# Where a two-layer graph-attention kernel asks whether its blocks hold all edges

## The chip, the cores and the metric

The kernel runs on one core of a Trainium2 chip. The metric is the device time of one execution in microseconds; the time before is the median of 3 runs. Beside it stands one execution taken by the hardware profiler, from which all durations are read.

## The reference

Two graph-attention layers over 3327 nodes with 1024 features, each with a residual and a layer norm. The adjacency matrix is sparse (a node has some 16 neighbours) and symmetric, with the diagonal set.

```python
h = x @ W                                    # layer 0: 8 heads of 128; layer 1: one head of 1024
e = leaky_relu(alpha_src[:, None] + alpha_dst[None, :], 0.2)
e = where(adj == 0, -inf, e)
out = softmax(e, axis=-1) @ h
x = layernorm(x + out)                       # layer 1: layernorm(x + relu(out))
```

## The kernel before, in words

The nodes are cut into 26 tiles of 128 rows (`NT = 26`, the last one partly filled). The program has three parts.

The first part is the stage "proj" (lines 453 to 699). For each tile, TensorE transposes x (`flip`, L176), multiplies it with the weights of layer 0 (`project`, L479), ScalarE copies the products out of PSUM (`keep`, L496), and SyncE writes them to the table `h0_d` in HBM (L499). Interleaved with this, the edges of each tile are turned into lists. The interleaving is written out by hand: `listing()` is a generator whose steps are called from `pace()` in the midst of the projections, so the order in each engine's queue is the order in which Python issues the instructions; nothing reorders them (`tc.manual_schedule()`). The steps that matter here:

- `words(t)` packs the adjacency rows and counts each node's edges (ScalarE L311, into `cnt[:, t, 0]`), four tiles ahead.
- `ends(t)` and `ends2(t)`, three tiles ahead of the lists, sum the counts over nodes: one small matmul each (L327, L346), a copy of it by ScalarE (L328, L347, into `cnt[:, t, 1]` and `cnt[:, t, 2]`) and a few small GpSimd operations.
- `keys` and `columns` find the column numbers of a tile's edges by repeated MAX8 and MATCH_REPLACE8 on VectorE (L274, L276).
- `places`, `give`, `take` and `sources` move these into blocks of edges: VectorE marks the places (L391, L392), TensorE permutes (L401, L411), ScalarE copies out (L423 to L428), and VectorE computes the index of each block's source rows (L436 to L450), into `idx`.

Behind the last list stands a question (L689 to L699): does every node have at most 32 edges, and does the spare block of each tile hold what is left over? VectorE scales the first count and copies the third into one tile `big`, reduces it to one number for each partition, TensorE transposes these 128 numbers (L695, into a PSUM bank of the tag "T", of which there are two, used in turn by `flip`, `ends`, `ends2` and this), VectorE reduces again and compares, and writes `flag`.

All five engines load the flag (L701) and branch on it (L1203). With the flag at 0, as with these inputs, the second part is `sparse`; the other arm, `by_pairs`, isn't run.

In `sparse`, layer 0 gathers the source rows of each tile's edges from `h0_d` with indirect DMAs from GpSimd (L803, four for each of four blocks and one for the spare block), VectorE makes the attention weights (L865 to L870), TensorE sums (L882 to L907), and the result is written to `y_d`. SyncE loads the lists' factors `re` (L812) and each tile's own rows (L838). Layer 1 does the same from `y_d` (L993), with its projection at the end (L1025).

The call that holds the order of the lists against the counts is in `listing`:

```python
                    if s == 3 and 2 < t + 3 < NT:
                        lists[t + 3].ends2(all_b)
                    yield
```

For t = 22 this is the last tile's second count; three lists (tiles 23, 24, 25) are then still to be finished.

Of the kernel before, what the change touches and what calls it, by code (L numbers as in the profile page):

```python
# [12 lines left out]
I32 = mybir.dt.int32  # L13
AF = mybir.ActivationFunctionType
OP = mybir.AluOpType
AX = mybir.AxisListType
# [3 lines left out]
P = 128  # L20
# [6 lines left out]
def kernel(  # L27
# [28 lines left out]
    nc = tc.nc  # L56
    N, D = x.shape
    H, DH = a0_src.shape
    NT = (N + P - 1) // P
# [8 lines left out]
    KMAX = 32  # L68
# [30 lines left out]
    const = ctx.enter_context(tc.tile_pool(name="const", bufs=1))  # L99
    scratch = ctx.enter_context(tc.tile_pool(name="scratch", bufs=1, space=DRAM))  # L100

    ident = const.tile([P, P], F32, name="ident")
# [10 lines left out]
    cnt = const.tile([P, NT, 3], F32, name="cnt")  # L113
# [43 lines left out]
    class Phase:  # L157
# [7 lines left out]
        def bank(self, tag, shape, name, dt=F32):  # L165
            return self.psum.tile(shape, dt, tag=tag, name=name, bufs=self.banks[tag])
# [286 lines left out]
    with ExitStack() as own, tc.manual_schedule():  # L453
        ph = Phase(own, "proj", {"A": 2, "S": 1, "T": 2})
        pool, bank = ph.pool, ph.bank
# [45 lines left out]
        def count(t):  # L501
            if t < NT:
                lists[t].words(ads.pop(t), junk)
                load_mask(t + 3)

        def listing():

            for t in range(-1, NT):
                old, new = lists[t] if t >= 0 else None, lists[t + 1] if t + 1 < NT else None
                for s in range(4):  # L510
                    if old:
                        old.give(s)
                    if new:
                        (new.keys, new.columns)[s // 2](s % 2)
                    if s == 1 and 2 < t + 3 < NT:
                        lists[t + 3].ends(tri_b)
                    if s == 3 and 2 < t + 3 < NT:
                        lists[t + 3].ends2(all_b)
                    yield
                if old:  # L520
                    old.give(EB)
                    old.take()
                count(t + 4)
                yield
                if old:
                    old.sources()
                    yield
                while new and t + 1 not in scored:
                    yield
                if new:  # L530
                    new.places()
                    yield

        scored, kept = set(), {}
        steps, slots, done = listing(), [0, 0], [0]

        def pace():
# [147 lines left out]
        for _ in steps:  # L685
            pass


        big = ph.sbuf("big", [P, NT, 2], 1)  # L689
        nc.vector.tensor_scalar(big[:, :, 0], cnt[:, :, 0], float(P) / KMAX, None, op0=OP.mult)  # L690
        nc.vector.tensor_copy(big[:, :, 1], cnt[:, :, 2])
        top = ph.sbuf("most", [P, 1], 1)
        nc.vector.tensor_reduce(top, big.rearrange("p a b -> p (a b)"), AX.X, OP.max)
        tr = bank("T", [1, P], "trc")
        nc.tensor.transpose(tr, top, ident)  # L695
        most = ph.sbuf("most1", [1, 1], 1)
        nc.vector.tensor_reduce(most, tr, AX.X, OP.max)
        flag = const.tile([1, 1], I32, name="flag")
        nc.vector.tensor_scalar(flag, most, float(P), None, op0=OP.is_gt)  # L699

    dense = nc.values_load(flag, min_val=0, max_val=1, skip_runtime_bounds_check_because="the result of a comparison")  # L701

# [529 lines left out]
```

## Time and profile before

| | us |
|---|---|
| median of 3 runs (1954.33 to 1958.33) | 1957.68 |
| the profiled execution | 1903.19 |
| its span, first to last instruction | 1901.5 |
| TensorE busy (share of the span) | 1518.5 (80%) |
| VectorE busy | 1146.6 (60%) |
| GpSimd busy | 1030.2 (54%) |
| ScalarE busy | 546.6 (29%) |

Times in the profile are in us from the first instruction. PE is TensorE's matmul queue, PEld its weight loads, DVE VectorE, ACT ScalarE, POOL GpSimd, SP SyncE, whose only work is to issue DMAs. A line such as L346 is a line of the kernel before. In the chain of waits each piece is work, or a wait for what released it; followed back from the last instruction, it tells what set the end. "issue" is time in which an engine waited for nothing that the profile shows. PEclk is the share of full clock that TensorE was granted. The ends of matmuls are modelled, so a gap of TensorE is known to some 0.1 us.

### The profile page before, as it was taken

What the parts mean: (1) busy time and instruction counts of PE and PEld (TensorE: products, weight loads), DVE (VectorE), ACT (ScalarE), POOL (GpSimd) and SP (SyncE); (2) the same over time, 40 slices, a digit from 0 to 9 for tenths busy, and PEclk for the clock granted to TensorE, in tenths of its full rate; (3) what the DMA queues carried; (4) which work ended last, traced back from release to release, by engine and by line L of the source; (5) the groups of instructions that cost most, each with busy time, mean ns of one, the idle gap of its engine ahead of it and who ended that gap; (6) DMA issues with size and microseconds to landing.
All of it is one profiled execution on the core that took longest, in us unless ns stands there. A gap on an engine that the chain in (4) does not pass through costs nothing.

```text
span 1901.5 us, 38079 instructions
## 1 busy us (share of the span) xinstructions
PE 1518.5 (80%) x14663; PEld 902.4 (47%) x14663; DVE 1146.6 (60%) x3058; ACT 546.6 (29%) x1422; POOL 1030.2 (54%) x1391
## 2 busy tenths in 40 slices
PE   8799999999266555656556565399999999999997
PEld 5465556666255554545545454144444444444443
DVE  6699999986386665666666666244444444444442
ACT  5544455542022222222222222012222212222220
POOL 4322222220576666676676764677766667666650
PEclk9899999999678777787788877699999999999999
DMA  7656455411899999999999997899999999999980
GB/s 184 101 133 131 100 99 99 88 62 39 325 373 404 396 392 394 366 405 392 386 392 389 394 376 273 332 398 410 400 372 382 380 378 369 359 371 373 366 326 33
DMA packets 171068, 567.76 MB, mean 299 GB/s; under 512 B 27690, under 2 KB 34346, under 8 KB 170878
## 3 DMA queue, kind: packets, MB, share of 16 engines
q0 software_dynamic: 131056, 455.68, 67.6%
q1 hardware_dynamic: 39822, 109.56, 15.4%
q8 instruction: 118, 1.93, 0.4%
q14 instruction: 72, 0.59, 0.1%
HBM read 578.85 MB, written 42.97 MB: 327 GB/s over the span
## 4 chain that ended last, share of the span: by engine, by line
PE 52%; DMA 24%; DVE 12%; ACT 6%; issue 4%; POOL 2%; SPq 0%; DVEq 0%; ACTq 0%; POOLq 0%
DMA src<-h_d,idx 20%; PE mm L1025 20%; PE acc L993 12%; PE mm L479 12%; DVE e L870 3%; PE acc L898 3%; ACT junk L311 3%; PE tr L176 2%; POOL src L803 2%; DMA src<-y_d,idx 2%; DVE pr L931 1%; PE acc L882 1%; DMA wt<-in_L_gnn_W_dram 1%; ACT xT L179 1%; PE xp L411 1%
## 5 line engine op out<-in xcount | busy, mean ns | idle before, releaser
L803 POOL DMA_INDIRECT src<-h_d,idx x416 | 441.1, 1060 | 209.1 <-PE acc L898 58.0
L803 POOL DMA_INDIRECT src<-y_d,idx x416 | 415.7, 999 | 221.6 <-PE acc L993 96.3
L898 PE MATMUL acc<-src,e 128*32 128x128 f32 x6656 | 278.5, 337 | 253.6 <-DVE e L870 253.5
L479 PE MATMUL mm<-wt,xT 128*128 128x347 f32 (+1 forms) x1248 | 402.3, 469 | 3.3 <-DMA wt<-in_L_gnn_W_dram 2.9
L1025 PE MATMUL mm<-wt,xT 128*128 128x512 f32 x832 | 383.3, 604 | 0.8 <-DVE o L1028 0.8
L898 PEld LDWEIGHTS acc<-src,e 128*32 128x32 f32 x6656 | 234.8, 137 | 311.3 <-DVE e L870 284.3
L479 PEld LDWEIGHTS mm<-wt,xT 128*128 128x128 f32 x1248 | 228.3, 192 | 106.0 <-issue 4.2
L1025 PEld LDWEIGHTS mm<-wt,xT 128*128 128x128 f32 x832 | 152.2, 190 | 199.5 <-issue 179.1
L993 PE MATMUL acc<-src,es 128*32 128x342 f32 (+1 forms) x2496 | 206.2, 464 | 33.8 <-DVE es L984 31.0
L870 DVE TENSOR_TENSOR e<-oh,way 128x1024 f32<-128x1024 f32 x130 | 158.7, 1221 | 63.2 <-ACT w L868 62.8
L993 PEld LDWEIGHTS acc<-src,es 128*32 128x32 f32 x2496 | 71.6, 111 | 158.6 <-issue 112.9
L868 ACT ACTIVATE w<-way 128x32 f32<-128x32 f32 (+1 forms) x130 | 24.6, 189 | 407.7 <-DVE way L866 395.6
L1028 DVE SCALAR_TENSOR_TENSOR o<-mm,y 128x512 f32<-128x512 f32 x52 | 35.9, 691 | 166.2 <-PE mm L1025 166.2
L1007 ACT ACTIVATE z<-y,ri 128x342 f32<-128x342 f32 (+1 forms) x78 | 39.5, 570 | 313.9 <-DVE ri L1003 313.9
L865 DVE TENSOR_TENSOR way<-src,re 128x32 f32<-128x32 f32 x104 | 20.8, 200 | 175.1 <-DMA src<-h_d,idx 157.6
L179 ACT ACTIVATE xT<-tr 128x512 f32<-128x512 f32 x104 | 59.4, 596 | 151.0 <-PE tr L176 150.9
L981 DVE TENSOR_TENSOR way<-way,src 128x128 f32<-128x128 f32 x104 | 31.1, 299 | 90.0 <-ACT way L951 44.2
L850 ACT ACTIVATE own<-own,es 128x128 f32<-128x128 f32 x208 | 63.6, 388 | 57.4 <-DVE es L847 57.4
L311 ACT ACTIVATE junk<-ad 128x3328 uint8<-128x3328 uint8 x26 | 78.4, 3014 | 2.5 <-POOL ad L308 2.5
L882 PE MATMUL acc<-end,e 128*128 128x128 f32 x416 | 67.7, 328 | 13.3 <-DVE e L870 13.3
L296 POOL CAST mvs<-r 128x8 bf16<-128x8 f32 x26 | 6.0, 232 | 122.8 <-ACT r L295 122.8
L335 POOL TENSOR_TENSOR place_of<-cnt 128x1 f32<-128x1 f32 x26 | 4.9, 190 | 121.0 <-ACT cnt L328 101.5
(188 smaller groups left out, 1959.7 us busy)
## 6 DMA issues: line engine op xcount, KB each, us to landing
h_d<-ht SPq DMA_DIRECT2D x26, 520.0 KB
own<-h_d SPq DMA_DIRECT2D x26, 520.0 KB
y_d<-y SPq DMA_DIRECT2D x26, 514.0 KB
y<-y_d SPq DMA_DIRECT2D x26, 514.0 KB
x<-in_x_dram SPq DMA_DIRECT2D x25, 512.0 KB
y<-in_x_dram SPq DMA_DIRECT2D x25, 512.0 KB
out_dram<-o SPq DMA_DIRECT2D x25, 512.0 KB
ad<-in_adj_dram POOLq DMA_DIRECT2D x25, 415.9 KB
```

Source lines behind the costliest of these rows:

```text
L176: nc.tensor.transpose(tr[:, k, :], src[:, (4 * g + k) * P : (4 * g + k + 1) * P], ident)
L179: nc.scalar.activation(part, tr, AF.Copy)
L311: nc.scalar.activation(junk, ad, AF.Copy, accum_out=self.deg)
L479: nc.tensor.matmul(acc, xT[t][:, k, :], wt[:, k, CUTS0[c] : CUTS0[c + 1]], start=k == 0, stop=k == KT - 1)
L803: nc.gpsimd.indirect_dma_start(out=s[:, g, :w], out_offset=None, in_=table[:, :], in_offset=bass.IndirectOffsetOnAxis(ap=idx[:, t, b * NG ...
L850: nc.scalar.activation(hn, hn, AF.Copy, scale=es[:, n : n + 1])
L870: nc.vector.tensor_tensor(e, oh.unsqueeze(2).to_broadcast([P, ng, H, wide]), wp.unsqueeze(3).to_broadcast([P, ng, H, wide]), OP.mult,)
L882: nc.tensor.matmul(self.acc[h // 4][:, h % 4, :], e[:, 0, h, :], rowsof[:, 0, h, :], start=False, stop=h % 4 == 3,)
L898: nc.tensor.matmul(self.acc[h // 4][g * GT : (g + 1) * GT, h % 4, :], e[:, g, h, :], rowsof[:, g, h, :], start=first and h % 4 == 0, stop= ...
L993: nc.tensor.matmul(self.acc[c][to, :m], es[:, g, :], s[:, g, CUTS[c] : CUTS[c + 1]], start=b == 0, stop=b == EB,)
L1007: nc.scalar.activation(z[:, cut], self.res[:, cut], AF.Copy, scale=ri[:, 1:2])
L1025: nc.tensor.matmul(acc, xT[:, k, :], wt1[:, k, half], start=k == 0, stop=k == KT - 1)
```

## The change

The operations of the question are put into a function `room()`, which is called in `listing` straight after `ends2` of the last tile. The block behind the last list is taken out. The load of the flag and the branch stay where they were, last in each engine's queue of the stage. Nothing else changes: on TensorE the transpose now stands between L346 and the eight transposes of the next `flip` (L176); on VectorE the five operations stand between the last MAX8 of tile 23's columns and L436 of tile 22; the queues of ScalarE, GpSimd and SyncE hold the same instructions in the same order.

```diff
                     if s == 3 and 2 < t + 3 < NT:
                         lists[t + 3].ends2(all_b)
+                        if t + 3 == NT - 1:
+                            room()
                     yield
...
+        flag = const.tile([1, 1], I32, name="flag")
+
+        def room():
+
+            big = ph.sbuf("big", [P, NT, 2], 1)
+            nc.vector.tensor_scalar(big[:, :, 0], cnt[:, :, 0], float(P) / KMAX, None, op0=OP.mult)
+            nc.vector.tensor_copy(big[:, :, 1], cnt[:, :, 2])
+            top = ph.sbuf("most", [P, 1], 1)
+            nc.vector.tensor_reduce(top, big.rearrange("p a b -> p (a b)"), AX.X, OP.max)
+            tr = bank("T", [1, P], "trc")
+            nc.tensor.transpose(tr, top, ident)
+            most = ph.sbuf("most1", [1, 1], 1)
+            nc.vector.tensor_reduce(most, tr, AX.X, OP.max)
+            nc.vector.tensor_scalar(flag, most, float(P), None, op0=OP.is_gt)
...
         for _ in steps:
             pass
 
-
-        big = ph.sbuf("big", [P, NT, 2], 1)
-        nc.vector.tensor_scalar(big[:, :, 0], cnt[:, :, 0], float(P) / KMAX, None, op0=OP.mult)
-        nc.vector.tensor_copy(big[:, :, 1], cnt[:, :, 2])
-        top = ph.sbuf("most", [P, 1], 1)
-        nc.vector.tensor_reduce(top, big.rearrange("p a b -> p (a b)"), AX.X, OP.max)
-        tr = bank("T", [1, P], "trc")
-        nc.tensor.transpose(tr, top, ident)
-        most = ph.sbuf("most1", [1, 1], 1)
-        nc.vector.tensor_reduce(most, tr, AX.X, OP.max)
-        flag = const.tile([1, 1], I32, name="flag")
-        nc.vector.tensor_scalar(flag, most, float(P), None, op0=OP.is_gt)
```

## The prediction

> **What bounds the kernel now.** I read the slices first, then the chain of waits around the hand-over between the two stages, then the timeline at the new place of the moved step, last busy time by window.
>
> The 40 slices (47.5 us each) of the page:
>
> ```profile
> PE   8799999999266555656556565399999999999997
> PEclk9899999999678777787788877699999999999999
> DMA  7656455411899999999999997899999999999980
> ```
>
> TensorE fills the first ten slices (the stage that projects x and makes the lists) and the last sixteen (second layer); between them, layer 0, DMA is full. The hand-over lies at the turn from slice ten to eleven. The chain of waits there:
>
> ```profile
> 473.61 1.37 PE mm L479 x4
> 474.98 0.01 PE xp L401
> ...
> 478.79 0.18 DVE idx L450
> 478.96 0.09 DVE big L690
> ...
> 480.16 0.15 DVE flag L699
> 480.31 0.02 issue
> 480.34 0.50 POOLq L701
> ...
> 482.35 1.15 POOL src L803
> ...
> 491.97 11.95 DMA src<-h_d,idx
> ```
>
> Start and length in us. The last projection ends at 474.98, the last list (L436 to L450) runs until 478.96 on VectorE, then come the five VectorE operations and the transpose of the question (L690 to L699) until 480.31; the flag is loaded, the branch taken, and the first gather starts at 482.35. From there the chain goes on through gathers (DMA 54% of the chain from 482 to 1200 us), so what moves the first gather moves the end.
>
> The timeline where the question is put in the changed kernel:
>
> ```profile
> 426.19 0.18 PE L346 MATMUL op<-more_b,all_b 128*128 128x1 bf16 x1
> 426.23 1.07 PE L176 MATMUL tr<-ident,x 128*128 128x128 f32 x8
> ...
> 428.76 0.43 DVE L274 MAX8 pack<-cols 128x8 f32<-128x256 f32 x1
> ...
> 429.22 0.19 DVE L436 TENSOR_TENSOR kq<-io_k,xs 128x16 f32<-128x16 f32 x1
> ```
>
> L346 is the matmul of the last tile's second count. TensorE goes straight on to eight transposes; VectorE is still in the top-k of an earlier tile and issues its last MAX8 2.57 us after L346. VectorE trails TensorE here.
>
> Busy us by window (TensorE, its weight loads, VectorE, ScalarE, GpSimd, granted clock, DMA share, GB/s), first around the early gaps of TensorE, then around the hand-over:
>
> ```profile
> 20.64:24.05 3.41, 1.39 (x9) 1.14 (x10) 3.38 (x4) 1.12 (x6) 2.62 (x2) 1.00 0.92 183
> 24.05:27.47 3.42, 3.42 (x10) 2.21 (x8) 3.38 (x4) 3.23 (x13) 0.28 (x1) 0.50 0.82 104
> 58.19:61.60 3.41, 1.54 (x7) 0.88 (x6) 3.13 (x11) 3.31 (x4) 0.61 (x2) 1.00 0.62 48
> 61.60:65.01 3.41, 2.46 (x18) 1.97 (x18) 2.63 (x8) 2.44 (x11) 2.45 (x14) 1.00 0.99 163
> ```
>
> ```profile
> 443.00:475.04 32.04, 32.04 (x208) 19.46 (x206) 18.20 (x52) 8.10 (x33) 1.64 (x8) 1.00 0.10 38
> 475.82:478.13 2.31, 0.00 (x0) 0.00 (x0) 2.02 (x5) 0.63 (x6) 0.00 (x0) 0.98 0.68 261
> ```
>
> A stretch of 3.41 us in which TensorE was busy for 1.39 us is followed by one at half clock; one with 1.54 us isn't. And from 443 to 475 TensorE has no gap (from 426.2 to 443 neither: 16.80 of 16.80): a stall put in there is given back nowhere.
>
> [...]SyncE branches at 480.91 and does its next instruction at 484.10, VectorE at 484.24, TensorE's branch takes 3.93 us[...]. [...]Here the last write of h0_d is issued until 475.82 and its last completion is recorded at 478.13, 2.31 us later.
>
> **What goes.** VectorE loses five operations from its tail, TensorE one transpose: 478.88 to 480.31, 1.4 us. No DMA is moved. The flag's load stays last in each engine's queue but finds its answer ready, so each engine branches when its own work ends: GpSimd 465.8, TensorE 475.0, ScalarE 476.4, SyncE 476.65, VectorE 478.96, against 480.34 for all. That isn't the gain. The first gather waits in the built program for all earlier writes of h0_d, not for the lists of other tiles; the last of these lands at 478.13. So the next wait is this landing, 478.13 against the 481.29 at which GpSimd came to that wait. From there to the gather's start the row of before has 1.05 us (three more waits, and the first gather's start-up). Whether that is paid after the landing, no row shows; the other end is two waits at 0.087 plus the 0.26 from a landing to a gather seen at 503.92, 0.43 us. I take 1.05, the only reading of this sequence. First gather, were nothing else changed: 478.13 + 1.05 = 479.18, **3.2 us earlier** (3.8 at the other end). This is all that the change can win.
>
> **What comes.** The same six operations stand behind L346 on TensorE and behind the last MAX8 on VectorE. The transpose (L695's) waits for VectorE's maximum, and behind it on TensorE is everything: the eight transposes L176, then the projections. Step by step: last MAX8 at 428.76; an independent operation follows a MAX8 after 0.35 (411.60 to 411.95), so the first at 429.11; from the first to the transpose 0.56 (478.88 to 479.44), so the transpose at 429.67; L176 one transpose later (0.11), 429.78 instead of 426.23. Its second half needs the bank that the transpose wrote, free when VectorE has reduced it: 0.69 after the transpose's start plus 0.05, 430.41, where before it stood at 426.70. **TensorE is 3.7 us late.** ScalarE's L347, which the operations read, is done at 426.57 and costs nothing. VectorE's reduction waits 0.41 us for the transpose with L436 queued behind it; L436 waits for ScalarE's xs, which waits for TensorE (L401), so it is late by the same 3.7 us and not more.
>
> The gap itself, 426.36 to 429.67, is 3.3 us. A window of 3.41 us is under the 1.4 us of busy time if about 2 us of the gap lie in it. Over the phases of the grid that holds for u < 1.35 or u > 1.95 of 3.41 (u: how much of the gap comes before the grid's mark), some 8 in 10; on the grid of this run a window is 426.83 to 430.24, with 2.8 us of gap. So I count **one window at half clock: 1.7 us** of projection lost (3.41 / 2). Its ends: nothing, or two windows, 3.4 us.
>
> **The sum.** TensorE late by 3.7 + 1.7 = 5.4 us; no gap follows, so the last projection ends at 480.4, h0_d lands at 478.13 + 5.4 = 483.5, first gather 483.5 + 1.05 = 484.6 against 482.35: **2.3 us later**. Beside it: SyncE's first load (the list weights re, which end the wait of VectorE's first L865 at 493.50) follows SyncE's own end, 476.65 + 5.4 = 482.1 against a flag at 480.33: 1.7 us later, under the gather's 2.3. VectorE ends at 484.4[...] and is done with its marks (1.3 us) by 490, before L865 at about 495.5; the gathers cover that, and without them it would cost 4 us. The profiled execution took 1903.19 us with a span of 1901.5; +2.3 gives 1905.5. It lies 54.5 us under the median of 1957.68, and no view says why; I add the shift to the median: **1960.0**. If the timed runs' TensorE is slower in this stage, VectorE trails less and the stall is shorter; the range takes that in.
>
> **Ends of the range.** VectorE's last MAX8 trails L346 by 1.58 to 3.80 us over the tiles from the fifth on (2.57 at the last). The stall is this plus 1.14: 2.7 to 4.9. Low: 2.7, no window, short start-up: 2.7 - 4.22 + 0.43 = -1.1. High: 4.9 + 3.4 - 4.22 + 1.05 = +5.2 (4.22 is 482.35 - 478.13). With about 1 us for the medians' own spread (runs lie between 1954.33 and 1958.33): 1955.5 to 1963.5.
>
> **Rivals.**
> - *Likeliest, as above, a small loss inside what can be told apart*: +0.9 to +3.9, 1960.0. Chance 0.60.
> - *A wash*: the stall comes, the clock holds. For it: the window with 1.54 us busy kept its clock[...]. Against: the gap is near a whole window. 3.7 - 4.22 + 1.05 = +0.5: 1958.2, down to -1.1. Chance 0.20.
> - *Slower*: one mechanism, the clock. The gap at L346 is long enough (VectorE trailing by 3.8, a gap of 4.5 us) that two windows run at half: +5.2, 1962.9. For it: the 7.3 us gap at 66 us was followed by three such windows. Against: that gap held an empty window. It decides when stall and half clock together pass 3.9 + 3.2 = 7.1 us. Chance 0.16.
> - *Faster*: the moved operations slip in without holding TensorE, since VectorE has caught up by then; then 3.2 to 3.8 us are won: 1954.2. Against: in all steady tiles VectorE is behind at L346. Chance 0.04.
> - That the change doesn't do what it says, the flag ready but no engine earlier, is half true already: GpSimd comes early and waits for h0_d.
>
> **Chances.** 0.2% of 1957.7 is 3.9 us, about what a measurement of this kernel can tell from no change. The likeliest case and the wash lie inside but for some spread at the upper edge: faster 0.04, within 0.76, slower 0.20.
>
> **What would show it.** A gap of TensorE of about 3.3 us before the transpose of the maximum, near 426.4 us; the granted clock at half for one 3.4 us window just after it; the last L479 ending near 480.4 instead of 475.0; GpSimd's branch far ahead of its first gather, and that gather about 1.2 us behind the landing of h0_d, near 484.6. Wrong would be: no gap at the transpose; a first gather before 482; or a first gather that moves while the end of the program doesn't follow, because layer 0 has slack that the chain doesn't show.

## The result, and the profile after

| | before | after |
|---|---|---|
| median | 1958.82 (22 runs) | 1964.13 (22 runs) |
| ratio of the comparable runs | | 1.0008, 95% interval 0.9992 to 1.0024 |
| the profiled execution | 1903.19 | 1963.96 |
| its span | 1901.5 | 1960.9 |

The change made no difference that can be told from none. The single runs scatter from 1952 to 1973 us, so the two medians differ by more (5.3 us) than the ratio says; the means, 1962.25 against 1960.64, lie as far apart as the ratio does. (One execution of the changed kernel, at 2231 us and a granted clock of 0.72 where the others show 0.91 or 0.92, is in the plain median but not in the means and the ratio.) By the ratio the change costs 1.6 us (-1.6 to +4.7); on the median of 1957.68 that is 1959.2, where 1960.0 was forecast. The plain median of 1964.13 lies 0.6 above the forecast range; before's own median had come out 1.1 higher in these runs than in the three of the forecast.

The two profiled spans differ by 59 us. That is not the change. The 40 slices of the changed kernel:

```profile
PE   8799999998477777777777776379999999999997
PEclk9899999999678898788888888689999999999999
DMA  7556554311999999999999995989999999999980
```

The first ten slices look as before; from the eleventh on TensorE is busy for 7 tenths instead of 5 or 6. By windows, layer 0 (first gather of h_d to first gather of y_d) takes 746.4 us against 716.2, with DMA moving 361 GB/s against 376, and layer 1 takes 729.0 against 702.9: 56 of the 59 us lie in stages that the change doesn't touch. The same kernel in a later set (e8_changed, below) has 712.1 and 701.4. So I compare times by ratios, and traces by the hand-over alone, counted from the matmul L346, which stands ahead of the moved question in every kernel.

The timeline of the changed kernel at the new place of the question (start, length, engine, line; in brackets the idle time before and what ended it):

```profile
426.85 0.18 PE L346 MATMUL op<-more_b,all_b 128*128 128x1 bf16 x1
...
429.43 0.43 DVE L274 MAX8 pack<-cols 128x8 f32<-128x256 f32 x1
429.78 0.16 DVE L541 TENSOR_SCALAR big<-cnt 128x26 f32<-128x26 f32 x1
...
430.42 0.37 PE L546 MATMUL trc<-ident,most 128*1 128x128 f32 x1 [3.39 <-DVE most L544]
...
430.63 1.94 PE L176 MATMUL tr<-ident,x 128*128 128x128 f32 x8
```

VectorE is still in an earlier tile's top-k when TensorE comes to the question; its last MAX8 starts 2.58 us after L346 (2.57 before the change). TensorE stands still for 3.39 us until VectorE's maximum is there, and eight transposes wait behind it. The windows from there on (length, busy us of TensorE, its weight loads, VectorE, ScalarE, GpSimd, granted clock, DMA share, GB/s):

```profile
426.80:430.21 3.41, 0.22 (x13) 0.11 (x5) 3.17 (x13) 0.52 (x2) 0.92 (x5) 1.00 0.39 159
430.21:433.63 3.42, 3.21 (x12) 2.63 (x13) 0.48 (x3) 1.20 (x2) 0.00 (x0) 0.50 0.01 2
```

The stretch with the gap has 0.22 us of matmuls in it, and the one after it runs at half clock. From 433.63 to 480.88 TensorE has no gap again. The chain of waits at the hand-over:

```profile
479.48 1.37 PE mm L479 x4
480.84 0.01 PE xp L401
480.86 0.02 issue
...
482.20 2.85 DMA re_d<-re
485.05 0.48 issue
485.53 1.15 POOL src L808
```

The question is gone from it. What stands there instead are transfers. The chain names the write of `re_d`, the last to end by the profile, but that isn't what held the gather: GpSimd's wait on the last write of `h0_d` lasts from 472.35 to 484.52, and its last wait on a write is over at 484.69, before `re_d` lands at 485.05. The write of `h0_d` landed at 484.49, 1.04 us before the gather. The branches (the line, its queue, its length, its start):

```profile
L1208 POOLq COMPARE_BRANCH  x1: 53/53/53, 472.0 to 472.0; - x1
L1208 PEldq COMPARE_BRANCH  x1: 3801/3801/3801, 479.9 to 479.9; - x1
```

GpSimd has branched at 472.0 and then waits some 12 us for the table. The hand-over side by side, in us from the start of L346:

| | before | after |
|---|---|---|
| last projection ends (last L401) | 48.85 | 54.06 |
| last write of h0_d, issue to landing | 2.63 | 3.12 |
| landing to first gather | 4.22 | 1.04 |
| first gather | 56.16 | 58.69 |

The gather is 2.53 us later: 5.21 us lost to TensorE, 0.5 to the landing, 3.2 won between landing and gather.

### The profile page after: what moved, and what is told of

Same layout as the page of the kernel before. It is cut to its first block, busy times and chain, and to the rows that moved or that the text cites. A ratio compares the mean times of both kernels' runs of the same rounds, so it can differ in the third digit from the quotient of the medians.

```text
span 1960.9 us, 38080 instructions
## 1 busy us (share of the span) xinstructions
PE 1656.4 (84%) x14663; PEld 932.7 (48%) x14663; DVE 1142.9 (58%) x3058; ACT 546.6 (28%) x1422; POOL 1033.2 (53%) x1391
## 4 chain that ended last, share of the span: by engine, by line
PE 73%; issue 12%; ACT 6%; DVE 5%; DMA 2%; another core or an unknown queue 1%; POOL 1%; SPq 0%; ACTq 0%; DVEq 0%
PE mm L1030 19%; PE acc L903 17%; PE acc L998 12%; PE mm L479 12%; PE acc L887 5%; ACT junk L311 3%; PE acc L895 3%; PE tr L176 3%; DMA wt<-in_L_gnn_W_dram 1%; PE den L912 1%; DMA src<-h_d,idx 1%; PE xp L411 1%; DVE top L274 1%; ACT xT L179 1%
## 5 line engine op out<-in xcount | busy, mean ns | idle before, releaser
L903 PE MATMUL acc<-src,e 128*32 128x128 f32 x6656 | 376.0, 294 | 171.7 <-issue 157.1
L479 PE MATMUL mm<-wt,xT 128*128 128x347 f32 (+1 forms) x1248 | 403.5, 469 | 4.0 <-DMA wt<-in_L_gnn_W_dram 3.6
L903 PEld LDWEIGHTS acc<-src,e 128*32 128x32 f32 x6656 | 228.2, 116 | 330.6 <-issue 291.2
L479 PEld LDWEIGHTS mm<-wt,xT 128*128 128x128 f32 x1248 | 228.7, 193 | 107.2 <-DMA wt<-in_L_gnn_W_dram 4.9
L998 PE MATMUL acc<-src,es 128*32 128x342 f32 (+1 forms) x2496 | 210.3, 465 | 40.5 <-DVE es L989 32.6
L887 PE MATMUL acc<-end,e 128*128 128x128 f32 x416 | 96.5, 425 | 1.8 <-DVE e L875 1.8
L887 PEld LDWEIGHTS acc<-end,e 128*128 128x128 f32 x416 | 89.1, 325 | 2.4 <-DVE e L875 1.8
L1006 DVE TENSOR_TENSOR ri<-acc,es 128x1 f32<-128x1 f32 x26 | 4.1, 158 | 111.4 <-PE acc L998 107.8
```

Source lines behind the costliest of these rows:

```text
L479: nc.tensor.matmul(acc, xT[t][:, k, :], wt[:, k, CUTS0[c] : CUTS0[c + 1]], start=k == 0, stop=k == KT - 1)
L887: nc.tensor.matmul(self.acc[h // 4][:, h % 4, :], e[:, 0, h, :], rowsof[:, 0, h, :], start=False, stop=h % 4 == 3,)
L903: nc.tensor.matmul(self.acc[h // 4][g * GT : (g + 1) * GT, h % 4, :], e[:, g, h, :], rowsof[:, g, h, :], start=first and h % 4 == 0, stop= ...
L998: nc.tensor.matmul(self.acc[c][to, :m], es[:, g, :], s[:, g, CUTS[c] : CUTS[c + 1]], start=b == 0, stop=b == EB,)
```

## Experiments

**Theory.** The early question costs a stall of TensorE of 3.7 us and one window at half clock, it wins some 3 us at the hand-over, and the difference goes into the time one for one. **Rivals:** the gain isn't there (another wait holds the gather in any case); layer 0 has slack, so that neither cost nor gain reaches the end; the end follows VectorE's first weights, or SyncE's first loads, and not the gather; VectorE catches up, so that only a first question stalls. Runs of one set were made on one chip, the sets on different chips (before: 1979.55, 1898.69 and 1897.67 us), so times are compared within a set.

### The gain without the stall (e1_split)

The maximum over the counts stays at the new place; the transpose and the comparison come with the next tile's list, 12.2 us after L346, when VectorE has long finished the maximum.

```diff
                         if t + 3 == NT - 1:
-                            room()
+                            largest()
+                    if s == 1 and t + 2 == NT - 1:
+                        room()
```

> The question in two halves: VectorE's maximum stays behind the last tile's second count, the transpose and what follows are asked one list later, when VectorE has long had the maximum. My theory (the change wins 3.2 us at the hand-over and loses 5.4 us on TensorE): no gap of TensorE at the transpose, no window at half clock before the hand-over, the last L479 ends 48.8 us after L346 as in the kernel before (54.0 in the changed one), and the first gather starts about 53.0 us after L346 (56.2 before, 58.7 changed); the time is 3 us under before, ratio 0.9984, at the edge of what can be told apart. Rival (GpSimd can't use an early flag, so that nothing is won): first gather 56 us after L346, ratio 1.000.

Measured: 0.9996 (0.9972 to 1.0021). TensorE's timeline of this kernel:

```profile
427.27 0.18 PE L346 MATMUL op<-more_b,all_b 128*128 128x1 bf16 x1
427.31 1.07 PE L176 MATMUL tr<-ident,x 128*128 128x128 f32 x8
```

There is no gap and no window at half clock; the last projection ends 48.86 us after L346, as before the change. The first gather comes at 53.40 instead of 56.16: 2.76 us won, under the 3.2 of the sum, since the landing takes 3.03 us instead of 2.63. The time's interval (some 5 us either way) is too wide to show 2.8 us; e9_split repeats it with more runs.

### The cost without the gain (e2_both)

The question is asked twice: at the new place into a word that nobody reads, and behind the last list, where it decides.

```diff
                         if t + 3 == NT - 1:
-                            room()
+                            room(early)
...
         for _ in steps:
             pass
+        room(flag)
```

> The question is asked twice: at the new place, into a flag that nobody reads, and again behind the last list, into the flag that counts. So it has the cost of the change without its gain. My theory: gap of TensorE 3.4 us, one window at half clock in most executions, last L479 54 us after L346, then the tail as before, first gather 61.6 us after L346 (56.2 before); the time is 5.4 us over before, ratio 1.0028. Rival (layer 0 has slack, and a few us at the hand-over don't reach the end): same gap and same late gather, ratio 1.000.

Measured: 1.0026 (1.0006 to 1.0047), that is +5.1 us. TensorE's gap is 3.38 us, one window runs at half clock, the last projection ends at 54.17 after L346 and the first gather at 61.49, 5.33 later than before. The cost is thus seen by itself, and it reaches the end. 5.33 less the 2.76 of e1_split makes 2.57, against 2.53 in the changed kernel: the two parts add up.

### The stall without the half clock (e3_filled)

24 transposes of the identity, which nothing uses, stand ahead of the question's transpose, so that TensorE is busy while it waits.

```diff
+            fill = bank("T", [P, 4, P], "fill")
+            for k in range(24):
+                nc.tensor.transpose(fill[:, k % 4, :], ident, ident)
             tr = bank("T", [1, P], "trc")
```

> As the changed kernel, with 24 transposes of the identity into a scratch bank ahead of the transpose that waits, so that TensorE is busy (for nothing) for 2.6 of the 3.4 us of the gap. My theory: TensorE still goes on only when VectorE has the maximum, but no window at half clock follows; last L479 52.5 us after L346 instead of 54.0, first gather 57.0 instead of 58.7; the time 0.8 us over before, ratio 1.0004. Rival (the half clock costs nothing by itself, since the stall alone makes the loss): the same 54.0 and 58.7 as the changed kernel.

Measured: 0.9992 (0.9972 to 1.0013). The windows, with the same columns as above:

```profile
426.70:430.10 3.40, 2.69 (x24) 2.31 (x23) 2.52 (x10) 0.23 (x1) 0.34 (x2) 1.00 0.40 161
430.10:433.50 3.40, 3.40 (x17) 2.28 (x16) 1.12 (x4) 1.99 (x8) 0.00 (x0) 1.00 0.00 1
```

2.69 us of matmuls instead of 0.22, and the clock holds in the next window. TensorE still waits 0.71 us after the fill, so the fill didn't delay the question. The first gather comes 57.11 us after L346, where 57.0 was put down. The last projection ends at 52.61 after L346: the stall alone is 52.61 - 48.85 = 3.76 us, and the half clock is 54.06 - 52.61 = 1.45 us. The time itself can't tell this kernel from the one before; the trace does the work here.

### The question four times (e4_four)

It is asked after each of the last four tiles' counts, over the tiles known by then; each answer overwrites the one before.

```diff
-                        if t + 3 == NT - 1:
-                            room()
+                        if t + 3 >= NT - 4:
+                            room(t + 4)
```

> The changed kernel with the question asked behind the second count of each of the last four tiles (over the tiles known by then; the last answer counts), so four stalls instead of one. In the kernel before VectorE's last MAX8 trails L346 by 1.8, 3.8, 1.9 and 2.6 us in these four. My theory: four gaps, together 10.1 + 4 x 1.14 = 14.6 us of stall, and one window at half clock after most of them, 4 x 1.7 = 6.8 us; less the 3.2 us of the early flag this is +18 us against before, ratio 1.009, clear of noise. Rival (VectorE catches up in the first stall and the later ones are short): first gap as in the changed kernel, later ones under 1 us, ratio under 1.004. Rival (slack in layer 0): gaps as my theory has them, ratio near 1.000.

Measured: 1.0073 (1.0049 to 1.0097), +14.4 us, where +18 was put down. Each of the four stalls TensorE (gaps of 2.55, 3.54, 2.70 and 2.80 us), and each is followed by a window at half clock. The third, with 1.40 us of matmuls in its window, shows how little idle time was enough here, 2.01 us:

```profile
420.13:423.54 3.41, 1.40 (x10) 1.19 (x11) 2.75 (x12) 0.61 (x2) 0.82 (x5) 1.00 0.38 156
423.54:426.95 3.41, 3.41 (x10) 1.96 (x9) 1.20 (x5) 1.81 (x8) 0.00 (x0) 0.50 0.00 0
```

VectorE's last MAX8 trails L346 by 1.8, 2.8, 1.9 and 2.0 us here, against 1.8, 3.8, 1.9 and 2.6 before. So VectorE catches up by 1 us in one stall and by 0.6 in another, which makes the loss smaller than forecast, but by far not as much as the rival needs. From L346 of the first tile that is asked about to L346 of the last it takes 61.8 us here and 47.9 before: 13.8 us for three stalls and three windows at half clock. With the last question's own net of 2.0 (first gather at 58.15 against 56.16) that is 15.8, inside the interval (9.7 to 19.2 us). The stage gives nothing back.

### The kernel before, once more (e5_again)

The same code in a second set, to see what a profile's scatter does to the hand-over.

> The kernel before, unchanged, as a run of its own: how far two sets of runs of one kernel lie apart, and how the execution profiled before (1903.19 us) stands among others. Ratio 1.000 within 0.002. At the hand-over: last L401 ends 48.8 us after L346, first gather 56.2 us after it, as in the first profile. If the first profile was an odd one out only in the layers, the first gather to the end takes some 1475 us here instead of its 1419; if the hand-over itself varies by microseconds from one execution to the next, its two figures move too, and the figures of the other experiments mean less.

Measured: 0.9997 (0.9988 to 1.0007). The first gather comes 56.16 us after L346 and the last projection ends at 48.85, both as in the first profile to 0.01 us. But the layers take 715.5 and 701.2 us here, as in the first profile (716.2 and 702.9), not the 762 and 728 of the trace of e1_split, nor the 1475 us in all that were put down for the case that the first profile was an odd one. It wasn't: on the chip of this set all executions are like the profile of 1903 us (median 1898.69).

### Does the gather's start reach the end? (e6_late and e7_late_split)

In e6_late, 32 multiplications that nothing uses (20 us of VectorE) stand ahead of the flag's comparison of the kernel before. In e7_late_split the same 32 stand in the split kernel, behind the last list, where VectorE is late but the flag isn't.

```diff
+        late = ph.sbuf("key", [P, WD], 1, "late")
+        nc.vector.memset(late, 1.0)
+        for _ in range(32):
+            nc.vector.tensor_tensor(late, late, late, OP.mult)
         flag = const.tile([1, 1], I32, name="flag")
         nc.vector.tensor_scalar(flag, most, float(P), None, op0=OP.is_gt)
```

> The kernel before with 32 dependent multiplications of a 128x416 tile on VectorE ahead of the flag's comparison, behind the last list: the hand-over is late by some 19 us (32 x 0.6), nothing else changes; they compute nothing that is used. My theory (what moves the first gather moves the end): the first gather 75 us after L346 instead of 56.2, the time over before by the full delay, ratio 1.0097. Rival (layer 0 has slack): the same late gather, ratio under 1.005.

> The same 32 multiplications behind the last list, with the question asked early in two halves as in the first experiment, so the flag doesn't wait for them. My theory (an early flag lets GpSimd go when h0_d has landed, whatever VectorE still does): first gather 53.4 us after L346 as in the first experiment, some 22 us earlier than with the late flag; VectorE reaches its first weights only about 78 us after L346, but the gathers fill their buffers until then, so most of the 19 us vanishes: ratio under 1.004 against before. Rival (the gathers alone are no gain, the end follows VectorE's first weights): ratio 1.006 or more, with the gather as early.

Measured, e6_late: 1.0102 (1.0086 to 1.0118), +19.4 us; the first gather came 20.3 us later (76.50 after L346). The chain of waits goes through the added work, from the question's transpose on:

```profile
479.12 0.39 PE trc L695
479.85 0.42 DVE late L699
480.29 0.60 DVE late L701
```

So there is no slack: what delays the hand-over delays the end. The late flag holds all five engines, so this run alone doesn't tell which of them the end follows; the next one takes VectorE apart from the gather.

e7_late_split: 0.9997 (0.9987 to 1.0006). Its first gather is as early as in e1_split (53.41), while VectorE comes so late that TensorE's first sums start at

```profile
511.45 3.58 PE L915 MATMUL acc<-src,e 128*32 128x128 f32 x64 [34.34 <-DVE es L863]
```

83.2 us after L346, where they stood at 69.5 before. Of 20.7 us of delay on VectorE, 13.7 of them left at TensorE's first sums, what the time shows is -0.6 us (-2.5 to +1.1) against the kernel before, or about 2 us if the 2.75 won by the gather are set against it. The end follows the gathers far more than VectorE's first weights.

### The change and the split again, and a version that wins more (e8_changed, e9_split, e10_ahead)

e8_changed is the changed kernel, e9_split the kernel of e1_split, both with more runs. In e10_ahead the split question is kept, and the next wait is shortened: the last tile's row of h0_d is written in three parts, each when its product is copied out, and its first two parts are projected without lists between, so that TensorE's last lists come after its last projection.

```diff
-            if kept[t] == 3:
+            if t == NT - 1:
+                cut = slice(c0, CUTS0[c + 1])
+                nc.sync.dma_start(h0_d[t * P : (t + 1) * P, cut], ht[:, cut])
+            elif kept[t] == 3:
                 nc.sync.dma_start(h0_d[t * P : (t + 1) * P, :], hts.pop(t))
...
             for c in (0, 1):
-                project(t, c)
+                project(t, c, t < NT - 1)
```

> The changed kernel once more, unchanged, beside the two below on one chip: does its loss of 2.5 us at the hand-over show in the time? My theory: last L401 54 us and first gather 58.7 us after L346 if the window at half clock falls into this execution too[...]; ratio between 1.0005 and 1.0015. Rival (a wash): ratio 1.000.

> The question in two halves once more (the maximum behind the last second count, the transpose one list later): first gather 53.4 us after L346, 2.8 us earlier than in the kernel before. My theory (the hand-over reaches the end one for one): ratio 0.9985. Rival (it gives no time back, since the first sums come only 1 us earlier): ratio 0.9995 to 1.000.

> Two halves as above, and the landing of h0_d moved forward as well: the last tile's row of h0_d is written in three pieces, each as soon as it is copied out of PSUM, and the last list's four groups of permutations (L411) stand behind the last projections instead of among them. My theory: the last L479 ends 0.75 us earlier after L346, the last write is a third of the bytes and lands some 0.8 us sooner after its issue, first gather 51.9 us after L346, 4.3 us earlier than before; ratio 0.9978. Rival (the landing isn't the wait that ends last, but GpSimd's own start): first gather at 53.4 as without it.

| | ratio, 95% interval | us by the ratio | first gather against before, from L346 |
|---|---|---|---|
| e8_changed | 1.0009 (1.0000 to 1.0018) | +1.7 | +2.47 |
| e9_split | 0.9987 (0.9980 to 0.9995) | -2.5 | -2.76 |
| e10_ahead | 0.9965 (0.9952 to 0.9979) | -6.6 | -5.31 |

The changed kernel's hand-over is the same as in its first trace (a gap of 3.38 us, one window at half clock, last projection at 54.08). The split one gains what the gather gains. These runs also set aside two rivals, again counted from L346. TensorE's first sums come 5.0 us later than before in e8_changed, and at the same time as before in e9_split (69.53 against 69.55), while the time of e9_split fell by 2.5 us. SyncE's first load of re comes 5.1 us earlier in e9_split (56.30 against 61.39), more than the time fell (0.9 to 3.8 us). Of the three, only the gather moved as the time did.

e10_ahead beats both kernels, and by more than I had put down: the last projection (L479) ends 1.45 us earlier than before, not 0.75, and the first gather starts at 50.85, not 51.9. Its chain of waits:

```profile
460.89 14.12 PE mm L479 x48
475.00 0.02 issue
475.03 0.47 ACT ht L496
475.50 0.02 issue
475.51 1.82 DMA h_d<-ht
...
478.50 1.59 POOL src L819
```

The last product's copy, its write and the gather follow on each other without a list between them, and the last part lands 1.82 us after its issue, where the whole row took 2.63 or more. Which of the two edits (three parts, no lists between) brings how much wasn't tried apart.

## Why the prediction was right, step by step

The sign, the size and the mechanism held: a small loss that can hardly be told from no change. The terms:

| step of the prediction | forecast | measured | where |
|---|---|---|---|
| TensorE's gap | 3.3 | 3.39 | after |
| stall of TensorE | 3.7 | 3.76 | e3_filled against before |
| one window at half clock | 1.7 | 1.45 | after against e3_filled |
| TensorE late in all | 5.4 | 5.2 | after against before |
| landing to first gather | 1.05 | 1.04 | after, e1_split, e8_changed |
| gain at the hand-over | 3.2 | 2.76 | e1_split, e9_split |
| first gather later by | 2.3 | 2.53 | after against before |
| share of it that reaches the end | all | all, within the intervals | e2_both, e6_late, e9_split |

- *The stall.* It was worked out from three rows of the kernel before (the trail of the last MAX8, the step after a MAX8, the five operations), and it held to 0.1 us, because the order of the queues is written by hand and the change left it alone elsewhere.
- *The half clock.* The reading from the trace of before, that 1.4 us of matmuls in a window are too few and 1.54 enough, held at each of the seven windows with an unfilled stall that I read (after, e2_both, e8_changed and the four of e4_four, with 0.07 to 1.40 us of matmuls in them); it held for e3_filled too, where filling the window to 2.69 us kept the clock. But as a threshold it is too sharp. In the stage of the lists, a window with 1.54 us kept its clock (before, from 58.19) and one with 1.70 us was followed by half clock (after, from 61.58). In the traces of before and after every change of the granted clock lies on a grid of 3.41 us; from the first record of the clock on (17.2 us) the two have 921 windows at full clock. Each of the 64 with under 1.42 us of matmuls was followed by half clock, none of the 762 with over 2.33 us was, and of the 95 between these 29 were. So a stall that leaves under 1.42 us in a window cost the next one in these traces, as forecast. The grid's next mark came 0.64 us after L346 before, 0.40 in e2_both and 3.36 in after, so where a gap falls on it differs from trace to trace, and the chance of 8 in 10 was an estimate over these places. It may have been too low, the window with 1.54 us spoke less for the wash than the prediction took it to, and one gap that falls evenly into two windows (some 1.7 us of work in each) could cost two, by my estimate from the window with 1.70 us. The price was put too high by a quarter of a us: 3.41 / 2 takes every us of the window to be lost by half. The window also holds the eight transposes, whose second half waits for the question's bank anyway, so that the two losses overlap; that fits, and wasn't tried by itself.
- *The gain.* Mis-sized by 0.4 us: the prediction moved the landing of before along with TensorE (478.13 + 5.4) and so took 2.63 us from issue to landing. With the early flag it is 2.99 to 3.12. In e2_both and e5_again, whose flag is late, it is 2.64. Why is not shown. In after fourteen of the write's 16 completions come by 2.64 us and the last two at 2.99 and 3.12, where before the change all 16 come between 2.48 and 2.63. What differs in time is TensorE's branch: in after it takes 3.80 us from 479.87, and the write is issued in the midst of it, at 481.37; before the change it takes 3.93 us from 480.94, behind the landing at 478.13. That the one slows the other is not shown. The shorter landing of e10_ahead (1.82 us) doesn't decide it, since its write is a third of the size.
- *The rivals.* "Wash" fell with the half clock. "Slower by two windows" fell with the trail, which was 2.58 us and not 3.8. "Faster" fell with the gap, but e9_split shows what it would have needed: a maximum that is ready when TensorE comes by. "Flag ready but no engine earlier" is half true, as said: GpSimd branched at 472.0 and still waited for the table.
- *What lies beside it.* SyncE read the flag 1.9 us later than before, counted from L346, where 1.7 was put down, but its first load of re came only 0.1 us later (61.53 against 61.39), well under the gather's shift; what took up the rest was not looked into. VectorE's lateness is hidden by the gathers, as the prediction argued: in e7_late_split 13.7 us of it cost about 2 us. The prediction's 490 for VectorE counts in the 3.9 us that VectorE stood still before the change between the flag (480.31) and its first work behind the branch (L753, 484.24); what fills them is not shown. GpSimd's first work behind its branch (L227) came 0.2 us after the branch, both before the change (480.91 to 481.14) and after it (471.97 to 472.20).
- *The 54.5 us* between the profile and the median, for which no view had a reason, go with the set of runs, and each set of the experiments had its own chip: layer 0 and layer 1 take 712 to 716 and 701 to 703 us in the first profile and on two chips, and 746 to 764 and 727 to 733 in the profile after and on a third chip, for the same code in these layers, with TensorE in layer 0 busy for 547 us against 419 (after against before). Whether it is the chip itself, and why, stays open. Adding the shift, and not the ratio, to the median was safe because the shift arises before those layers.
- *A reading that was off.* The 40 slices show TensorE full in the last fourteen, not the last sixteen. Nothing in the sum rests on it.

Open: the time itself confirms the loss only barely (+1.6 and +1.7 us, the one interval holding zero and the other touching it). That there is a loss rests on the traces and on e2_both and e6_late, where the same path was loaded more.

## What to carry to other kernels

Before a question that goes from one engine to another and back is moved, look whether its producer is ahead at the new place: here VectorE trailed by 2.6 us, and the full engine behind the question paid 3.8 us for it and 1.45 for the clock. Cut in two, with the producer's half early and the full engine's half one list later, the step cost TensorE nothing. Then look for the wait that is next (here the landing of the table's last rows): removing one wait won 2.8 us at the gather's start, shortening the next another 2.5.

## What had not been expected of the hardware

- In the traces of before and after, a window of 3.41 us at full clock was followed by one at half clock each of the 64 times that it held under 1.42 us of matmuls, none of the 762 times that it held over 2.33 us, and 29 of the 95 times in between: 1.42 us kept the clock (before, from 829.60), 2.33 us didn't (after, from 805.68).
- A write of 520 KB landed 2.63 or 2.64 us after its issue in the traces with the late flag (before, e2_both, e5_again) and after 2.99 to 3.12 us in those with the early one (after, e1_split, e3_filled, e8_changed, e9_split); a third of it, in e10_ahead, after 1.82 us. In after only the last two of the write's 16 completions came late, at 2.99 and 3.12 us; the others came by 2.64.
- The time from the table's landing to the first gather's start was 1.04 us in all of these with an early flag, and 1.17 in e10_ahead, where the last write's semaphore stands in the first of the gather's four waits and not in the second: it came behind the landing although GpSimd was there early (in after, it had waited since 472.35 for the landing at 484.49).
- The hand-over repeated to 0.06 us between sets of runs (last projection and first gather 48.85 and 56.16 us after L346 in before and in e5_again, 54.06 and 58.69 in after, 54.08 and 58.63 in e8_changed), while the gathering layers behind it differed by 3 to 7% (712 to 716 against 746 to 764 us, and 701 to 703 against 727 to 733).
